# A GAT layer and a relational attention layer in one kernel: the order of the four score quads within a turn

## The chip, the cores and the metric

The kernel runs on one core of a Trainium2 chip. The metric is device time in microseconds (us) for one execution of the whole program. The program works in float32 throughout. The engines are called by the profile's names: PE (matmuls; PEld are its weight loads), DVE (vector), ACT (scalar activations), POOL (GpSimd) and SP, which here only issues DMAs.

## The reference, cut to what matters

64 graphs of 256 nodes with 256 features pass through two layers. Layer 0 is a graph attention (two attention steps, then a norm, a feed-forward of width 1024 and a norm); layer 1 is an attention with 8 heads whose weights pass through masks by relation, followed again by norm, feed-forward and norm.

```python
# layer 1, the part around the change (adj is 0 or 1 here, so two relations count)
q = (src @ Wq + bq), k = (src @ Wk + bk)          # 8 heads of 32
attn = softmax(einsum('bhid,bhjd->bhij', q, k) / sqrt(32))
for r in range(R):
    v_r = src @ Wv[r] + bv[r]
    out = out + einsum('bhij,bhjd->bhid', attn * (adj == r), v_r)
x = _ln(src + out @ Wo + bo, g1, beta1)
# layer 0's feed-forward, of the graphs that come next
h = _layernorm(residual + h, g_ln1, b_ln1)
ff = relu(h @ w_ff1 + b_ff1) @ w_ff2 + b_ff2
h = _layernorm(h + ff, g_ln2, b_ln2)
```

## The kernel before, in words

Two graphs are one group, so there are 32 groups. A stretch of the program, `turn(y_, x_, z)` (L1154), takes one group `y_` through the attention and the second feed-forward, the next group `x_` through its first feed-forward, and the one after that, `z`, through the two graph attention steps. The three are interleaved by hand. Inside a turn the order on PE, SP, DVE and ACT is the order of the Python calls (`tc.manual_schedule`, L1195, with all four engines while there is an `x_`); POOL is not among them. An engine executes in that order and waits where an input or a buffer isn't ready.

The steps that the change moves:

- **Scores, `scores(n)`** (L1164, in `weighted`, L1006). A quad is four heads of one graph; a turn has four: quads 0 and 1 for graph 0, quads 2 and 3 for graph 1. The 16 matmul instructions `sp` (L1015) contract over 32 rows each, so that four of them stand side by side in the rows of the array (32*128 in the profile); they write four PSUM banks. ACT then takes the exponential of each bank (L1021).
- **Masks and totals, `masks(n)`, `totals(n)`** (L1026, L1031): DVE multiplies the exponentials by the adjacency, two heads at a time, and adds both halves for the denominators.
- **Sums, `sums(n)`** (`applied`, L1034): 32 matmuls `po` (L1041) and 8 matmuls `zo` (L1044) with 32 output columns each, four side by side in the columns of the array (128*32). They need the masks, the totals and the values of their graph.
- **Values, `values`** (L992): per block of 128 nodes four matmul instructions of 512 columns (`vp`, L999), then a DVE add into `v` (L1001). Blocks 0 and 1 belong to graph 0, blocks 2 and 3 to graph 1.
- **Feed-forward steps, `first("2a 1a ...")`** (`hidden_seven`, L842, steps in L892). The first matrix product of the feed-forward is done with seven products (Strassen's way) for each half a and b of the hidden units. Steps 2, 5 and 3 use one PSUM bank (`h1b`) and are copied by ACT (L880); steps 1, 6, 7 and 4 use the other (`h1a`), the first three added by DVE (L883). Each step is four matmul instructions (L871). As they run in one bank one after the other, step 5a has to wait for the copy of 2a, 3a for the copy of 5a, 6a for the add of 1a, 7a for that of 6a, 4a for that of 7a. "r" and "s" are activations on ACT alone. Four subtractions (L854) on DVE prepare the moving operands; they wait for the DMAs `hT<-yt` (L687) that place the transposed features.
- **Shares, `shares(b)`** (`divided`, L1047): DVE transposes the denominators, inverts them, transposes back and multiplies `po` by them (L1052 to L1057); the PSUM tiles `po` and `zo` have one buffer each, so graph 1's sums wait for graph 0's shares.
- **`early(z)`** (L1064): a DVE transposition of the input of group `z`; **`project(z, ...)`** (L1074): its projection `xpp` on PE (L715), copied by ACT; **`plus(X["y"], rb1)`** (L839): the shift of the first norm, a DVE addition over 128x1024 elements; **`applied_norm(waiting...)`** (L818): four ACT activations (L828) after a small DVE one (L821), for the group that is leaving.

All matmul results but `po` and `zo` go to one rotating set of six PSUM banks (`bank`, L423): a new tile takes the bank that came free first and waits for its last reader.

Of the kernel before, what the change touches and what calls it, by code (L numbers as in the profile page):

```python
# [12 lines left out]
ALU = mybir.AluOpType  # L13
# [3 lines left out]
P = 128  # L17
# [368 lines left out]
def narrow_path(  # L386
# [13 lines left out]
    nc = tc.nc  # L400
    B, N, F = x.shape
# [7 lines left out]
    T = G * NB  # L409
# [13 lines left out]
    def bank(name):  # L423
        return psum.tile([P, 512], F32, tag="g", name=name, bufs=6)
# [4 lines left out]
    def load_x(u):  # L429


        xq = io.tile([P, KB, TN], F32, tag="xq", name=f"xq{u}", bufs=1)
        xu = x[G * u:G * (u + 1)].rearrange("b (n r) (k q c) -> q k r (b n) c", r=32, k=KB, c=32)
        for q in range(Q):
            for k in range(KB):
                nc.sync.dma_start(xq[q * 32:(q + 1) * 32, k, :].rearrange("r (n c) -> r n c", c=32), xu[q, k])
        g[u].update(xq=xq)
# [65 lines left out]
    def row(v, name, t=None):  # L503
        n = v.shape[0]
        if t is None:
            t = const.tile([P, n], F32, name=name)
        nc.sync.dma_start(t, bass.AP(tensor=v.tensor, offset=v.offset, ap=[[0, P], [1, n]]))
        return t
# [41 lines left out]
    rg1, rb1, rg2, rb2 = row(g_g1, "rg1"), row(g_b1, "rb1"), row(g_g2, "rg2"), row(g_b2, "rb2")  # L550
# [267 lines left out]
    def applied_norm(y, blocks, mv, rs, nm, part=None, gpsimd=False):  # L818
        bt = slice(blocks[0], blocks[0] + len(blocks))
        if part is None or part[0] == blocks[0]:  # L820
            nc.vector.scalar_tensor_tensor(nm[:, bt], mv[:, bt, 0], -1.0, rs[:, bt],  # L821
                                           op0=ALU.mult, op1=ALU.mult)
        for t in part or blocks:
            if gpsimd:
                nc.gpsimd.tensor_scalar(y[:, t, :], y[:, t, :], rs[:, t:t + 1], nm[:, t:t + 1],
                                        op0=ALU.mult, op1=ALU.add)
                continue
            mark["normed"] = nc.scalar.activation(y[:, t, :], y[:, t, :], AF.Identity,  # L828
                                                  bias=nm[:, t:t + 1], scale=rs[:, t:t + 1])
# [6 lines left out]
    def times(y, g_):  # L836
        nc.vector.tensor_mul(y, y, g_[:, None, :].to_broadcast(list(y.shape)))  # L837

    def plus(y, b_):  # L839
        nc.vector.tensor_add(y, y, b_[:, None, :].to_broadcast(list(y.shape)))  # L840
# [134 lines left out]
    def out_sums(u, l):  # L975
        two = [work.tile([P, HPB, NB * N], F32, tag=t, name=f"{t}q{u}_{l}") for t in ("e", "ea")]
        return [t[:, :, i * N:(i + 1) * N] for t in two for i in range(2)]
# [14 lines left out]
    def values(u, hT, blocks, v=None):  # L992
        if v is None:
            v = work.tile([P, T, 2 * F], F32, tag="v", name=f"v{u}", bufs=1)
        wvf = wv.rearrange("p c r f -> p c (r f)")
        for t in blocks:
            ps = bank(f"vp{u}_{t}")
            for k in range(KB):
                nc.tensor.matmul(ps, hT[k][:, t * P:(t + 1) * P], wvf[:, k, :],  # L999
                                 start=(k == 0), stop=(k == KB - 1))  # L1000
            nc.vector.tensor_tensor(v[:, t, :], ps, rbv, ALU.add)  # L1001
        return v
# [21 lines left out]
    def masked(b, m, ab, e, ea, pairs=(0, 2)):  # L1024
        for a in pairs:
            nc.vector.tensor_tensor(ea[:, a:a + 2, :], e[:, a:a + 2, :],  # L1026
                                    ab[:, None, :].to_broadcast([P, 2, NB * N]), ALU.mult)
# [19 lines left out]
    def divided(u, b, po, zo, oT):  # L1047


        rz = work.tile([P, KB * N], F32, tag="s" if u < NG - 1 else "yt", name=f"rz{u}_{b}", bufs=1)  # L1050
        rq = work.tile([P, KB * N // 32], F32, tag="rq", name=f"rq{u}_{b}")
        nc.vector.transpose(rz, zo)  # L1052
        nc.vector.reciprocal(rq, rz.rearrange("p (n r) -> p n r", r=32)[:, :, 0])  # L1053
        nc.gpsimd.tensor_add(low, low, rq)  # L1054
        nc.vector.transpose(rz.rearrange("p (n r) -> p n r", r=32),
                            rq[:, :, None].to_broadcast([P, KB * N // 32, 32]))
        mark[f"divided{b}"] = nc.vector.tensor_tensor(  # L1057
            oT[:, :, b * N:(b + 1) * N], po.rearrange("p (m n) -> p m n", m=KB),
            rz.rearrange("p (m n) -> p m n", m=KB), ALU.mult)
# [4 lines left out]
    def early(z):  # L1064

        d = g[z]
        xT = work.tile([P, KB, TN], F32, tag="hT", name=f"xT{z}")
        nc.vector.transpose(xT.rearrange("p k n -> p (k n)"), d["xq"].rearrange("p k n -> p (k n)"))
        d["xT"] = [xT[:, k] for k in range(KB)]
# [4 lines left out]
    def project(z, blocks=range(T)):  # L1074
        d = g[z]
        d["xp"] = projected(z, d["xT"], blocks, d.get("xp"))
# [73 lines left out]
    def piece():  # L1150
        if left:
            next(left[0], None)

    def turn(y_, x_, z):  # L1154
        Y, X, Z = (g.get(u) for u in (y_, x_, z))
        hT, y = Y["hT"], Y["y"]
# [3 lines left out]
        oT = q  # L1160
        acc = [None] * G
        e = {}

        def scores(n):  # L1164
            e[n] = weighted(y_, *quads[n], q, k_, Y["aT"])

        def masks(n, *pairs):
            masked(*e[n], *pairs)

        def totals(n):  # L1170
            e[n] = node_sums(*e[n])

        def sums(n):
            b, m = quads[n]
            if m == 0:
                acc[b] = [psum.tile([P, 512], F32, tag=t_, name=f"{t_}{y_}_{b}") for t_ in ("po", "zo")]
            applied(b, m, v, *e.pop(n), *acc[b])

        def shares(b):
            divided(y_, b, *acc[b], oT)  # L1180

        def out_(b):
            add_blocks(y_, "yop", y, b, lambda t, k: oT[:, k, t * P:(t + 1) * P],
# [2 lines left out]
        def first(names, ends=0):  # L1186

            if X:
                steps(names)
            else:  # L1190
                for _ in range(ends):
                    piece()
# [4 lines left out]
        with order:  # L1197
# [4 lines left out]
            last = norm(waiting[0][0], 3, waiting[0][1]) if waiting else None  # L1202
            key(0)
            key(1)
            if X:
                X["hT"] = normed_features(x_, 0, X["y"])
                times(X["y"], rg1)
            scores(0)
            if z + 1 < NG:
                load_x(z + 1)  # L1210
            if X:
                masks(0)
                totals(0)
            v = values(y_, hT, range(0, T // 2))
            if not X:
                masks(0)
                totals(0)
            if waiting:
                applied_norm(waiting[0][1], *last)
            if X:  # L1220
                v = values(y_, hT, range(T // 2, T), v)
            steps = first_hidden(x_) if X else None
            scores(1)
            if not X:
                v = values(y_, hT, range(T // 2, T), v)
            if Z:
                early(z)
            masks(1)
            totals(1)
            sums(0)  # L1230
            first("2a 1a 5a", 1)
            scores(2)
            sums(1)
            if X:
                shares(0)
            first("3a 6a", 1)
            if not X:
                with behind("out"):
                    shares(0)
            masks(2, (0,))  # L1240
            first("2b 1b")
            masks(2, (2,))
            first("5b 7a 3b ra 6b")
            totals(2)
            first("4a 7b rb")
            if X:
                plus(X["y"], rb1)
            scores(3)
            first("sa sb", 2)
            masks(3)  # L1250
            totals(3)
            if Z:
                project(z, range(0, T // 2))
            first("4b")
            sums(2)
            sums(3)
            if not Z:
                shares(1)
            if X:
                out = HiddenOut(x_, 0, X["y"], X["h1"], wf2s, out_sums(x_, 0))  # L1260
                if Z:
                    out.sums(1, 2)
            if Z:
                shares(1)
            out_(0)
            mv = moments(y_, 2, y, range(NB))
            piece()
# [2 lines left out]
            if Z:  # L1270
                early_adjacency(z)
            elif X:
                out.sums(1)
                out(1, 2)
                out.sums(2)
            out_(1)
# [21 lines left out]
            if X:  # L1298
# [3 lines left out]
                if Z:  # L1302
                    hT = normed_features(y_, 2, y, queues=(nc.sync, nc.scalar))
# [4 lines left out]
            if not Z:  # L1308
                piece()
                hT = to_features(y, f"h3T{y_}")  # L1310
                hT = [h.rearrange("p (t a r) -> p t a r", t=T, r=32) for h in hT]
# [52 lines left out]
            out = HiddenOut(y_, 1, y, h1, w2s, out_sums(y_, 1))  # L1364
# [26 lines left out]
    waiting = []  # L1391

    with tc.manual_schedule(engines={mybir.EngineType.PE, mybir.EngineType.SP}):
# [23 lines left out]
        first = HiddenOut(0, 0, g[0]["y"], g[0]["h1"], wf2s, out_sums(0, 0))  # L1417
# [63 lines left out]
```

## Time and profile before

| what | value |
|---|---|
| five runs, median (lowest to highest) | 3074.53 us (3073.17 to 3076.09) |
| the profiled execution | 3074.8 us |
| its span, from first to last instruction | 3073.2 us |
| granted clock of PE | 0.994 |
| PE / PEld / DVE / ACT / POOL busy | 3033.1 / 2330.7 / 2596.0 / 1601.1 / 642.6 us |
| one turn, first `qp` matmul to the next turn's | 93.43 us (for example 1321.09 to 1414.52) |

The profiled execution's own time lies 1.6 us above its span, and 0.3 us above the median. Times in the text such as 1328.05 are microseconds from the start of the span, in one turn in the middle of it. In the timeline a line gives the start, the time from the first start to the last end, the engine, the source line and the operation with its tiles, and in brackets how long the engine was idle before and who ended that. In the chain of waits a line gives the start and how long the chain ran through that piece of work. PE's matmuls overlap at their ends, so the distance from one block's start to the next one's is what a block costs.

### The profile page before, as it was taken

How to read it: one execution, taken by the hardware profiler on the slowest of the kernel's cores; microseconds unless marked ns; L12 is line 12 of the kernel's file. 1: busy time of each engine (PE TensorE's matmuls, PEld its weight loads, DVE VectorE, ACT ScalarE, POOL GpSimd, SP SyncE). 2: the span in 40 equal slices, each digit the busy share in tenths (PEclk: the TensorE clock that was granted, in tenths of full speed). 3: DMA queues.
4: the chain of work that ended last, by engine and by line, in shares of the span. 5: the costliest groups of instructions: out<-in, count | busy, mean ns of one | idle time of the engine just before them, and what ended most of it. 6: DMA issues, size and time to landing. Idle time of an engine off the chain costs nothing.

```text
span 3073.2 us, 56408 instructions
## 1 busy us (share of the span) xinstructions
PE 3033.1 (99%) x21432; PEld 2330.7 (76%) x21432; DVE 2596.0 (84%) x4886; ACT 1601.1 (52%) x3212; POOL 642.6 (21%) x888
## 2 busy tenths in 40 slices
PE   7999999999999999999999999999999999999998
PEld 6677877778777778777778777787777787777866
DVE  4788888888888888888888888888888888888876
ACT  4455555555545555545555455555455555555553
POOL 3122121222211221211221112222112212122200
PEclk8999999999999999999999999999999999999999
DMA  5011111221111211111211112111112111121000
GB/s 149 13 37 36 33 39 25 44 44 32 36 40 25 44 37 36 35 29 40 44 35 34 39 25 44 40 36 34 35 32 44 37 33 39 25 44 37 19 13 16
DMA packets 427988, 113.37 MB, mean 37 GB/s; under 512 B 364568, under 2 KB 427072, under 8 KB 427712
## 3 DMA queue, kind: packets, MB, share of 16 engines
q1 hardware_dynamic: 417664, 102.46, 15.8%
q10 hardware_dynamic: 8992, 6.19, 0.9%
q8 instruction: 172, 2.82, 0.4%
q0 software_dynamic: 1056, 1.05, 0.1%
q14 instruction: 104, 0.85, 0.1%
HBM read 57.04 MB, written 16.78 MB: 24 GB/s over the span
## 4 chain that ended last, share of the span: by engine, by line
PE 91%; DVE 7%; DMA 1%; ACT 1%; POOL 0%; issue 0%; SPq 0%; ACTq 0%; POOLq 0%; DVEq 0%
PE yf L960 22%; PE h1a L871 15%; PE h1b L871 11%; PE po L1041 8%; PE vp L999 7%; PE sp L1015 4%; PE xpp L715 4%; PE qp L986 4%; PE kp L986 4%; PE yop L786 4%; PE ygp L786 3%; PE hpp L775 2%; PE zo L1044 2%; DVE s L750 2%; DVE yt L668 1%; DVE eaq L946 1%
## 5 line engine op out<-in xcount | busy, mean ns | idle before, releaser
L880 ACT COPY h<-h1b 128x512 f32<-128x512 f32 x384 | 224.2, 584 | 390.9 <-PE h1b L871 390.9
L883 DVE TENSOR_TENSOR h<-h1a,h 128x512 f32<-128x512 f32 x384 | 263.6, 687 | 117.5 <-PE h1a L871 111.9
L828 ACT ACTIVATE y<-y,nm,rs 128x256 f32<-128x256 f32 x450 | 238.7, 591 | 238.3 <-DVE nm L821 234.0
L1026 DVE TENSOR_TENSOR ea<-e,aT 128x1024 f32<-128x1024 f32 x256 | 309.3, 1238 | 55.0 <-ACT e L1021 55.0
L1021 ACT ACTIVATE e<-sp 128x512 f32<-128x512 f32 x512 | 264.4, 604 | 52.0 <-PE sp L1015 48.7
L1054 POOL TENSOR_TENSOR low<-low,rq 128x16 f32<-128x16 f32 x64 | 13.8, 216 | 1088.6 <-DVE rq L1053 1088.6
L685 POOL COPY hT<-yt 32x256 f32<-32x256 f32 x244 | 206.2, 845 | 59.4 <-DVE yt L668 51.8
L968 DVE TENSOR_TENSOR y<-yf,y 128x256 f32<-128x256 f32 x448 | 183.1, 409 | 40.2 <-PE yf L960 40.1
L999 PE MATMUL vp<-wv,hT 128*128 128x512 f32 x480 | 214.0, 599 | 0.0
L801 DVE BATCH_NORM_STATS2 st<-y 128x6 f32<-128x256 f32 x512 | 207.8, 408 | 5.6
L812 POOL TENSOR_SCALAR rs<-mv 128x4 f32<-128x4 f32 (+1 forms) x130 | 31.2, 240 | 729.7 <-DVE mv L802 471.0
L999 PEld LDWEIGHTS vp<-wv,hT 128*128 128x128 f32 x480 | 88.7, 190 | 110.4 <-issue 103.2
L840 DVE TENSOR_TENSOR y<-y,rb 128x1024 f32<-128x1024 f32 (+1 forms) x130 | 166.5, 1281 | 3.2
L988 ACT ACTIVATE q<-qp,cols 128x512 f32<-128x512 f32 x64 | 44.0, 687 | 240.3 <-PE qp L986 240.3
L914 ACT ACTIVATE h<-h,cols 128x512 f32<-128x512 f32 x256 | 167.0, 714 | 1.5 <-DVE h L883 1.1
L837 DVE TENSOR_TENSOR y<-y,rg 128x1024 f32<-128x1024 f32 (+1 forms) x130 | 161.9, 1245 | 2.2 <-ACT y L828 1.1
L1031 DVE TENSOR_TENSOR es<-e 128x1024 f32<-128x1024 f32 x128 | 155.5, 1215 | 0.0
L677 POOL COPY hT<-yt 32x256 f32<-32x256 f32 x120 | 116.1, 968 | 169.5 <-DVE yt L668 165.7
L1015 PEld LDWEIGHTS sp<-q,k 32*128 32x128 f32 x2048 | 92.5, 184 | 72.1 <-issue 44.8
L1015 PE MATMUL sp<-q,k 32*128 32x256 f32 x2048 | 146.6, 400 | 0.0
L1041 PE MATMUL po<-e,v 128*32 128x256 f32 x2048 | 136.3, 384 | 0.0
L668 DVE STREAM_TRANSPOSE yt<-y 128x256 f32<-128x256 f32 x364 | 129.6, 412 | 7.4 <-ACT y L828 6.1
(249 smaller groups left out, 7196.5 us busy)
## 6 DMA issues: line engine op xcount, KB each, us to landing
hT<-yt SPq DMA_DIRECT2D x912, 32.0 KB, 2.0
y<-in_x_dram SPq DMA_DIRECT2D x32, 512.0 KB, 5.1
xq<-in_x_dram SPq DMA_DIRECT2D x240, 64.0 KB, 2.1
aq<-in_adj_dram SPq DMA_DIRECT2D x240, 64.0 KB, 2.4
out_dram<-y SPq DMA_DIRECT2D x30, 512.0 KB, 2.9
hT<-yt ACTq DMA_DIRECT2D x180, 32.0 KB, 1.9
wf<-in_L_gnn_w_ff_dram SPq DMA_DIRECT2D x2, 1024.0 KB, 7.1
w<-in_L_gnn_W_dram SPq DMA_DIRECT2D x2, 1024.0 KB
```

The lines of the kernel that those rows point to most:

```text
L786: nc.tensor.matmul(ps[:, i * F:(i + 1) * F], lhs(t, k), rhs(b, k), start=(k == 0), stop=(k == n - 1))
L828: mark["normed"] = nc.scalar.activation(y[:, t, :], y[:, t, :], AF.Identity, bias=nm[:, t:t + 1], scale=rs[:, t:t + 1])
L871: nc.tensor.matmul(ps[:, i * N:(i + 1) * N], w_[:, f * P:(f + 1) * P], m, start=first and i == 0, stop=True, skip_group_check=True)
L880: mark["copied"] = nc.scalar.copy(out(h, o, b), pair(ps))
L883: mark["added"] = nc.vector.tensor_tensor(out(h, o, b), pair(one[h]), out(h, o, b), ALU.add)
L960: nc.tensor.matmul(s.ps[n][:, i * F2:(i + 1) * F2], a[:, k, i * P:(i + 1) * P], w_[:, k, :], start=n in (1, 2, 5) and i == 0 and k == 0, s ...
L986: nc.tensor.matmul(ps, w[:, k, m * P:(m + 1) * P], hT[k], start=(k == 0), stop=(k == KB - 1))
L999: nc.tensor.matmul(ps, hT[k][:, t * P:(t + 1) * P], wvf[:, k, :], start=(k == 0), stop=(k == KB - 1))
L1015: nc.tensor.matmul(ps[a][:, j * N:(j + 1) * N], k_[hp, m, j0:j0 + P], q[hp, m, b * N:(b + 1) * N], start=True, stop=True)
L1021: mark[f"exp{b * KB + m}"] = nc.scalar.activation(e[:, a, :], ps[a], AF.Exp, scale=isd)
L1026: nc.vector.tensor_tensor(ea[:, a:a + 2, :], e[:, a:a + 2, :], ab[:, None, :].to_broadcast([P, 2, NB * N]), ALU.mult)
L1041: nc.tensor.matmul(po[hp, m * N:(m + 1) * N], vs[:, hp], w[:, a, j * N:(j + 1) * N], start=(n == 0), stop=(n == len(terms) - 1))
```

## The change

On PE, a turn that has both an `x_` and a `z` (30 of the 32) ran, from the first scores on: scores 0, values 0 to 3, scores 1, sums 0, steps 2a 1a 5a, scores 2, sums 1, steps 3a 6a 2b 1b 5b 7a 3b 6b 4a 7b, scores 3, two projections, step 4b, sums 2 and 3. It now runs: scores 0, values 0 to 2, scores 1, sums 0, scores 2, steps 2a 1a 2b 5a, values 3, steps 3a 6a, sums 1, scores 3, steps 5b 7a 1b 3b 6b 4a 7b, two projections, step 4b, sums 2 and 3.

On DVE, the totals, masks, the transposition of `early` and the shares take new places between the adds of the steps; the shares of graph 0 are split in two by a `yield`. The addition of `rb1` leaves DVE: POOL issues a DMA that adds `rb1` to `X["y"]` in SBUF, early in the turn. The group that is leaving gets its norm activations ahead of masks 0.

```diff
         nc.gpsimd.tensor_add(low, low, rq)
+        yield
         nc.vector.transpose(rz.rearrange("p (n r) -> p n r", r=32),
...
                 times(X["y"], rg1)
+                nc.gpsimd.dma_start(X["y"], rb1[:, None, :].to_broadcast([P, T, F]), accum_op=ALU.add)
             scores(0)
             if z + 1 < NG:
                 load_x(z + 1)
+            if waiting:
+                applied_norm(waiting[0][1], *last)
...
-                v = values(y_, hT, range(T // 2, T), v)
+                v = values(y_, hT, range(T // 2, T - 1), v)
             steps = first_hidden(x_) if X else None
             scores(1)
...
-            if Z:
-                early(z)
             masks(1)
-            totals(1)
+            if not X:
+                totals(1)
             sums(0)
-            first("2a 1a 5a", 1)
-            scores(2)
-            sums(1)
             if X:
-                shares(0)
-            first("3a 6a", 1)
-            if not X:
+                scores(2)
+                first("2a 1a")
+                totals(1)
+                first("2b")
+                masks(2, (0,))
+                first("5a")
+                v = values(y_, hT, range(T - 1, T), v)
+                first("3a 6a")
+                masks(2, (2,))
+                sums(1)
+                scores(3)
+                first("5b")
+                totals(2)
+                if Z:
+                    early(z)
+                first("7a 1b")
+                divide = shares(0)
+                next(divide)
+                first("ra 3b 6b")
+                next(divide, None)
+                first("4a 7b")
+                if Z:
+                    project(z, range(0, T // 2))
+                first("rb")
+                first("sa sb")
...
-            masks(2, (0,))
-            first("2b 1b")
-            masks(2, (2,))
-            first("5b 7a 3b ra 6b")
-            totals(2)
-            first("4a 7b rb")
-            if X:
-                plus(X["y"], rb1)
-            scores(3)
-            first("sa sb", 2)
             masks(3)
             totals(3)
-            if Z:
-                project(z, range(0, T // 2))
             first("4b")
             sums(2)
             sums(3)
```

The last two turns keep an order of their own: turn 30 has no `z`, so `early` and `project` fall away in it, and turn 31 has no `x_` either. After sums 3 the calls `out.sums(1)` and `out.sums(2)` now stand ahead of the second `shares` in every turn with an `x_`.

More of the change, by code (lines that the diff above doesn't have):

```diff
@@ L1179, in shares @@
         def shares(b):
-            divided(y_, b, *acc[b], oT)
+            return divided(y_, b, *acc[b], oT)
         def out_(b):
@@ L1217, in turn @@
                 totals(0)
-            if waiting:
-                applied_norm(waiting[0][1], *last)
             if X:
-                v = values(y_, hT, range(T // 2, T), v)
+                v = values(y_, hT, range(T // 2, T - 1), v)
             steps = first_hidden(x_) if X else None
@@ L1225, in turn @@
                 v = values(y_, hT, range(T // 2, T), v)
-            if Z:
-                early(z)
             masks(1)
-            totals(1)
+            if not X:
+                totals(1)
             sums(0)
-            first("2a 1a 5a", 1)
-            scores(2)
-            sums(1)
             if X:
-                shares(0)
-            first("3a 6a", 1)
-            if not X:
-                with behind("out"):
-                    shares(0)
-            masks(2, (0,))
-            first("2b 1b")
-            masks(2, (2,))
-            first("5b 7a 3b ra 6b")
-            totals(2)
-            first("4a 7b rb")
-            if X:
-                plus(X["y"], rb1)
-            scores(3)
-            first("sa sb", 2)
+                scores(2)
[23 more added lines that the diff above has]
+                first("sa sb")
+            else:
+                piece()
+                scores(2)
+                sums(1)
+                piece()
+                with behind("out"):
+                    for _ in shares(0):
+                        pass
+                masks(2)
+                totals(2)
+                scores(3)
+                piece()
+                piece()
             masks(3)
             totals(3)
-            if Z:
-                project(z, range(0, T // 2))
             first("4b")
@@ L1256, in turn @@
             sums(3)
-            if not Z:
-                shares(1)
             if X:
                 out = HiddenOut(x_, 0, X["y"], X["h1"], wf2s, out_sums(x_, 0))
+                out.sums(1)
                 if Z:
-                    out.sums(1, 2)
-            if Z:
-                shares(1)
+                    out.sums(2)
+            for _ in shares(1):
+                pass
             out_(0)
@@ L1272, in turn @@
             elif X:
-                out.sums(1)
                 out(1, 2)
```

## The prediction

> **What bounds the kernel now.** I read the page's busy times first, then the chain of waits, then PE's and DVE's timelines in one turn.
>
> ```profile
> PE 3033.1 (99%) x21432; PEld 2330.7 (76%) x21432; DVE 2596.0 (84%) x4886; ACT 1601.1 (52%) x3212; POOL 642.6 (21%) x888
> ...
> PE 91%; DVE 7%; DMA 1%; ACT 1%; POOL 0%; issue 0%; SPq 0%; ACTq 0%; POOLq 0%; DVEq 0%
> ```
>
> PE is busy for 99% and is 91% of the chain that ended last. DVE at 84% is no bound; it counts only where PE waits for one of its results. So a change of order can win or lose just two things: what PE loses between blocks, and PE's short waits. The chain of waits in one turn shows both (start, length, block):
>
> ```profile
> 1328.12 1.08 PE sp L1015 x16
> 1329.20 7.06 PE vp L999 x16
> 1336.26 1.08 PE sp L1015 x16
> 1337.34 1.86 PE po L1041 x32
> 1339.20 0.43 PE zo L1044 x8
> 1339.63 1.06 PE h1b L871 x4
> 1340.69 0.86 PE h1a L871 x4
> 1341.56 0.94 PE h1b L871 x4
> 1342.50 1.08 PE sp L1015 x16
> ...
> 1352.28 2.85 PE h1a L871 x12
> 1355.12 1.08 PE sp L1015 x16
> 1356.20 1.95 PE xpp L715 x8
> ```
>
> A feed-forward step costs 0.86 where nothing disturbs it. The first one behind `zo` costs 1.06. Sixteen scores, four abreast, are also four steps of work (0.86) and cost 1.08. The 32 `po` behind scores cost 1.86; the same 32 behind another quad's `zo` cost 1.73 (at 1361.31). The projection costs 1.95 behind scores and 1.75 elsewhere (at 1365.39). So each time PE goes from one division of the array to another it loses about 0.20 into a full-array block, 0.13 into `po` and 0.22 into scores.
>
> The second loss: step 5a takes 0.94, and so do 5b and 3b; each waits for an ACT copy of its bank, and its weights load late (0.08 each). Steps 6b, 4a and 7b take 2.85 in place of 2.59: 7b waits for DVE's add of 6b (0.25).
>
> **The change part by part**, for one turn, 30 of which have the full new order.
>
> *Divisions of the array.* Before, the stretch from scores 0 to the output product enters scores 4 times, `po` 3 times and full blocks 5 times (values, 2a, 3a, projection, output product). After, scores 2 and 3 follow `zo` directly: scores are entered 4 times, `po` 3 times, full blocks 4 times (values, 2a behind scores 2, 5b behind scores 3, output product). One entry goes: **-0.20**. This assumes that scores cost 1.08 behind `zo` as they do behind a full block. The trace has no scores directly behind `zo`. Bounds: 0.86, their bare work, if that entry is free (-0.22 each), and 1.30, twice the entry, if both divisions had to be paid (+0.22 each); two such places, so -0.44 to +0.44 a turn. I take 1.08, the nearest row: scores cost it in all four places, whatever stood ahead.
>
> *Values 3 behind scores 1.* Scores 1 come 1.72 sooner (4 of 16 matmuls, 6.88 / 4). Four of six banks are needed. In the order in which banks come free these are those of scores 0 (heads 1 to 3) and that of values 0, where before they were heads 2 and 3 and values 0 and 1. DVE frees it late:
>
> ```profile
> 1327.91 1.23 DVE L837 TENSOR_TENSOR y<-y,rg 128x1024 f32<-128x1024 f32 x1
> 1330.33 2.56 DVE L1026 TENSOR_TENSOR ea<-e,aT 128x1024 f32<-128x1024 f32 x2 [1.20 <-ACT e L1021]
> 1332.82 1.21 DVE L1031 TENSOR_TENSOR es<-e 128x1024 f32<-128x1024 f32 x1
> 1333.96 1.27 DVE L1001 TENSOR_TENSOR v<-vp,rbv 128x512 f32<-128x512 f32 x2
> ```
>
> Values 0 are added from 1333.96 to 1333.96 + 0.68 = 1334.64 (0.68 is the single add of L1001). PE would be ready for scores 1 at 1336.19 - 1.72 = 1334.47 and, with some 0.05 from DVE's end to PE's start (at 7b DVE ends at 1353.93 and PE's weights start at 1353.99), begins at 1334.69: **+0.21**. All of PE stands behind it. Bounds: 0 if the add is that much sooner; 0.8 if the bank is values 1's, added 0.6 later.
>
> *Waits of the steps.* I laid the new order out with the durations above: every instruction starts when its engine is free and its inputs are there. Scores 2 start at 1338.05 and their four exponentials (0.49 apart) hold ACT to 1341.0; the copy of 2a ends at 1341.6. Step 2b now stands ahead of 5a, which is due at 1341.8: its weights load late (0.07). Later 3b and 6b each load late by 0.07 to 0.09, 7b still waits 0.25 for the add of 6b. Sum 0.48; before 0.08 + 0.08 + 0.08 + 0.25 = 0.49. **About 0.** Values 3 stand in front of 3a and take its wait away.
>
> *DVE.* `plus` (1.22) goes; the rest is the same work in new places. DVE ends totals 3 at about 1360.6, against 1360.9 before, and sums 3 want them only at 1363, so nothing is gained: scores 3's exponentials and the step adds set its pace. The shares of graph 0 end at 1356.6, sums 2 need them at 1358.9. The subtractions wait for the DMAs `hT<-yt` until 1337.42 as before; step 2a, which reads the same tile, comes at 1339.1, so a cover of 1.7 is left. Ahead of masks 0 stands a new DVE instruction of 0.15, in DVE's 1.20 of idle time. **0.**
>
> *ACT.* The projection's copies now stand ahead of "rb" and "s", which end some 0.6 later; behind them wait the sums `eq` on DVE and graph 1's shares, done at 1366.2; the output product that reads them starts at 1366.98. **0**, cover 0.7.
>
> *SP.* Its queue holds the next load of `xq` until `early` has read the buffer: 1340.16 now, some 10 us later after. The next entries are wanted 30 us later. **0.**
>
> *The accumulating DMA.* Its sum is read by the first add of the feed-forward's output, over 35 us later; the only DMAs that POOL issues before took 8.1 us to land. Hidden. But POOL must issue it, behind its four copies (1327.99 to 1330.7), beside DVE's masks 0. That masks pair took 2.56, with the copies beside its first half (1.43); the pair at 1340.05, alone, took 2.31. The two POOL issues in the trace take 1.0 and 0.8. So between 0 and +0.22 on masks 0, and on scores 1 as they wait for values 0 behind them. I take 0: the copies read and write 256 elements on each of 32 partitions, an issue moves no tile.
>
> The Trainium skill, SBUF — State Buffer, section "Who interferes with whom", says that a DVE instruction with two SBUF inputs contends with a GpSimd instruction that reads SBUF, not with one that only writes it; the copies agree (0.39 alone, 1.38 beside the multiplication by `rg`). If making the descriptors is only writing, the term is 0 by the page; if it also reads, the page would have it as the +0.22 above.
>
> Sum: -0.20 + 0.21 + 0 = +0.01 a turn, 0.3 us over 30 turns. In turn 30 nothing stands between 7b and 4b any more, which costs about 1 us, and the missing `plus` gives about as much back where DVE is the bound there. The profiled execution (3074.8, span 3073.2 + 1.6) gives 3075.1; the median of the runs is 0.3 lower. I say **3075.0**.
>
> **The rivals.** About 0.2% (6 us, 0.2 a turn) is what a measurement of this kernel can tell from no change.
>
> *Faster.* Scores behind `zo` cost less than behind a full block, or DVE frees the bank in time. For it: into `po` PE loses only 0.13, so entries differ. Against: 1.08 at every place. With half the entry saved (-0.11 twice) and no wait at scores 1 the sum is -0.20 - 0.22 = -0.42, times 30 is -13: **3062**. Either one alone gives 3068 to 3069.
>
> *Slower: DVE is late at values 0.* POOL's issue stretches masks 0 by 0.22, PE waits 0.43 instead of 0.21 at scores 1, 30 x 0.22 = 6.6: **3082**. It decides once values 0's add ends after 1334.47, which it already does here, so every delay counts in full. With values 1's bank, +0.6 a turn: 3093.
>
> *Slower: the divisions are dear.* 1.30 for scores behind `zo`: 30 x 0.44 = 13: **3088**. It is in the range's upper end.
>
> *The order isn't what the diff says.* On PE, DVE and ACT it is written out by hand; only POOL's place for its DMA is free. I give this nothing.
>
> **How the numbers follow.** No change that can be told (3069 to 3081) 0.46; faster 0.32 (the best known term is a saving, the added waits are each a matter of 0.1 to 0.2); slower 0.22 (late DVE 0.15, dear divisions or another bank 0.07). The range leaves out half of each far case: 3062 to 3084. The likeliest case's own range is 3069 to 3081.
>
> **What would show it.** In PE's timeline: 1.08 from scores 2's start to 2a's, with 2.29 ahead of it from `po` to scores; the entry behind `zo` read off as any excess. A wait of 0.2 ahead of scores 1, with DVE's L1001 as its releaser. L840 gone from the group of 130 by about 31, a DMA issued by POOL in each turn, where the trace now has two in all. Masks 0 at 2.56 again, or longer. A turn of 93.4. The prediction is wrong if scores behind `zo` differ from 1.08 by over 0.1, if scores 1 wait 0 or over 0.4, or if 5a waits for ACT's copy by over 0.2.

## The result and the profile after

The changed kernel took 3081.1 us (median of 23 runs, 3077.4 to 3083.5); before, run beside it, 3075.1 (43 runs, 3071.9 to 3077.5). The ratio is 1.0020, 95% interval 1.0014 to 1.0025: **slower by 6.0 us, 0.2%**, at the border between "no change" and "slower". The forecast was 3075.0 with a range of 3062 to 3084. The profiled execution took 3082.5, its span is 3080.8; the granted clock of PE is 0.994, as before.

From the page of the kernel after, busy times and the chain's shares:

```profile
PE 3034.5 (98%) x21432; PEld 2339.8 (76%) x21432; DVE 2560.2 (83%) x4855; ACT 1601.0 (52%) x3212; POOL 684.3 (22%) x919
...
PE 87%; DVE 8%; ACT 1%; DMA 1%; SPq 1%; POOL 1%; issue 1%; DVEq 0%; ACTq 0%; POOLq 0%
```

DVE has lost 35.8 us and 31 instructions: `plus` is gone. POOL has gained 41.7 us and 31: the issues of the DMA. PE's work is the same, but SP's queue and POOL now appear in the chain that ended last, each with 1%. The chain of waits of the kernel after, in the turn from 1327.14 to 1420.67 (start, length, block):

```profile
1340.60 1.27 PE sp L1015 x14
1341.87 1.86 PE po L1041 x32
1343.73 0.43 PE zo L1044 x8
1344.16 1.08 PE sp L1015 x16
1345.24 1.06 PE h1b L871 x4
...
1347.16 1.87 PE h1b L871 x8
...
1358.64 1.01 PE h1b L871 x4
1359.64 2.89 PE h1a L871 x12
```

Scores directly behind `zo` cost 1.08, and the step behind them 1.06, as behind any other block. Scores 1 cost 1.27: a wait of 0.19 inside them (the chain's line counts 14 of their 16 matmuls). The pairs and triples of steps have their small waits: 1.87 where two steps' bare work is 1.72, 1.01 for 0.86, 2.89 for 2.59. This turn is 93.53 long, before 93.44; most turns are like it. DVE's timeline in the same turn, masks 0 and the adds of values 0 to 2:

```profile
1336.38 2.57 DVE L1026 TENSOR_TENSOR ea<-e,aT 128x1024 f32<-128x1024 f32 x2 [0.93 <-ACT e L1021]
...
1340.01 1.87 DVE L1001 TENSOR_TENSOR v<-vp,rbv 128x512 f32<-128x512 f32 x3
```

Masks 0 are as long as before. The first add begins at 1340.01 and takes 0.68, to 1340.69, while scores 1 are on PE from 1340.53 on.

In ten of turns 1 to 29, and in turn 30, step 2a starts late. Here is one of these, the turn from 1233.07 to 1327.14, in the chain and then in DVE's timeline (in brackets the idle time before and its releaser):

```profile
1250.09 1.08 PE sp L1015 x16
1251.17 0.65 issue
1251.82 1.10 PE h1b L871 x4
```

```profile
1251.70 0.42 DVE L854 TENSOR_TENSOR tt<-hT 128x256 f32<-128x256 f32 x1 [3.89 <-DMA hT<-yt]
```

PE stands still for 0.65, and DVE has waited 3.89 for the transposed features. They landed just before both could start. The chain calls PE's gap "issue", a time for which it found no releaser; DVE's line, 0.12 earlier and about the same tile, names it. In the totals of this line over the whole trace DVE's idle time behind `hT<-yt` goes from 20.9 us (24 times) to 101.6 (44 times). Most of that costs nothing, as DVE has less to do there without `plus`: in dma_later below it is 63.6 (44 times), and no step 2a comes late. SP's timeline shows where the delay begins. First the kernel before, then the kernel after, each with the twelve issues of one turn as one line (first start, time to the last end); then POOL's timeline of the kernel after, in the same turn:

```profile
1328.01 7.55 SPq L687 DMA_DIRECT2D hT<-yt  x12
```

```profile
1334.06 9.16 SPq L687 DMA_DIRECT2D hT<-yt  x12
```

```profile
1334.04 2.70 POOL L685 COPY hT<-yt 32x256 f32<-32x256 f32 x4 [0.23 <-DVE yt L668]
1336.69 1.35 POOL L1209 DMA_DIRECT2D y<-rb  x1
```

Twelve issues take 9.16 where they took 7.55. One by one, as medians over turns 1 to 28: each lasts 0.59 before; after, the eighth and the ninth last 1.10, and they begin 11.35 and 12.51 into the turn. POOL's issue runs from 9.55 to 10.90, and the accumulating DMA lands at 14.83. So two of SP's issues stretch while that DMA moves its 512 KB. The last issue comes at 14.94 instead of 13.88, and the subtractions start at 17.57 (up to 18.63) instead of 16.15; step 2a is due at 18.03.

### The profile page after: what moved, and what is told of

Its sections match the earlier page's. It is cut to its first block, busy times and chain, and to the rows that moved or that the text cites. A ratio compares the mean times of both kernels' runs of the same rounds, so it can differ in the third digit from the quotient of the medians.

```text
span 3080.8 us, 56471 instructions
## 1 busy us (share of the span) xinstructions
PE 3034.5 (98%) x21432; PEld 2339.8 (76%) x21432; DVE 2560.2 (83%) x4855; ACT 1601.0 (52%) x3212; POOL 684.3 (22%) x919
## 4 chain that ended last, share of the span: by engine, by line
PE 87%; DVE 8%; ACT 1%; DMA 1%; SPq 1%; POOL 1%; issue 1%; DVEq 0%; ACTq 0%; POOLq 0%
PE yf L960 21%; PE h1a L871 14%; PE h1b L871 11%; PE po L1041 7%; PE vp L999 7%; PE sp L1015 4%; PE yop L786 4%; PE xpp L715 4%; PE ygp L786 3%; PE qp L986 3%; PE kp L986 3%; PE hpp L775 2%; PE zo L1044 2%; DVE s L750 2%; DVE eaq L946 1%; DVE yt L668 1%
## 5 line engine op out<-in xcount | busy, mean ns | idle before, releaser
L1015 PE MATMUL sp<-q,k 32*128 32x256 f32 x2048 | 153.0, 400 | 1.2 <-ACT k L988 1.2
L717 ACT COPY xp<-xpp 128x260 f32<-128x260 f32 x128 | 48.0, 375 | 195.7 <-PE xpp L715 195.7
L854 DVE TENSOR_TENSOR tt<-hT 128x256 f32<-128x256 f32 x122 | 51.4, 421 | 105.7 <-DMA hT<-yt 101.6
```

The costliest lines, as they stand in the source:

```text
L1015: nc.tensor.matmul(ps[a][:, j * N:(j + 1) * N], k_[hp, m, j0:j0 + P], q[hp, m, b * N:(b + 1) * N], start=True, stop=True)
```

## The experiments

Theory 1 in the expectations: the accumulating DMA holds up the transfers of `hT`, and 2a waits for them. Theory A: scores 1 wait for the bank of values 0 because totals 0 stand ahead of their add on DVE. All kernels side by side; "turn" is the usual (median) turn of turns 1 to 29, "long" the number of turns over that by more than 0.12 us, the next two columns are medians from the start of a turn, "turn 30" is its length:

| kernel | time | ratio to before on the same chip | turn | long | last `hT` issue | subtractions | turn 30 |
|---|---|---|---|---|---|---|---|
| before | 3075.1 | 1 | 93.44 | 5 | 13.88 | 16.15 | 74.12 |
| after | 3081.1 | 1.0020 (1.0014 to 1.0025) | 93.53 | 7 | 14.94 | 17.57 | 75.60 |
| plus_on_dve | 3077.5 | 1.0008 (0.9999 to 1.0017) | 93.55 | 1 | 13.89 | 16.20 | 75.22 |
| totals_later | 3077.3 | 1.0006 (0.9997 to 1.0015) | 93.35 | 11 | 14.94 | 17.61 | 75.82 |
| both | 3072.1 | 0.9991 (0.9982 to 1.0000) | 93.34 | 2 | 13.90 | 16.24 | 75.02 |
| dma_alone | 3077.6 | 1.0005 (0.9996 to 1.0014) | 93.44 | 8 | 14.98 | 17.23 | 74.17 |
| scores3_apart | 3080.6 | 1.0010 (1.0001 to 1.0019) | 93.53 | 1 | 13.89 | 16.23 | 75.21 |
| values_back | 3103.1 | 1.0085 (1.0070 to 1.0100) | 94.27 | 1 | 13.89 | 16.95 | 75.95 |
| shares_at_once | 3105.4 | 1.0093 (1.0078 to 1.0109) | 94.33 | 4 | 13.90 | 16.24 | 75.99 |
| last_as_before | 3073.4 | 0.9989 (0.9980 to 0.9998) | 93.33 | 3 | 13.90 | 16.24 | 74.14 |
| dma_later | 3072.7 | 0.9989 (0.9980 to 0.9998) | 93.33 | 3 | 13.89 | 16.21 | 74.17 |

The kernel before took 3075.3 beside plus_on_dve to dma_alone, 3076.6 beside scores3_apart to last_as_before, and 3076.1 beside dma_later. The first 102 to 107 us, ahead of turn 0, differ by that much between single traces although the code there is the same; so turns, and not spans, are compared.

**plus_on_dve**: the kernel after, with `rb1` added by DVE, in its idle time ahead of the subtractions.

```diff
-                nc.gpsimd.dma_start(X["y"], rb1[:, None, :].to_broadcast([P, T, F]), accum_op=ALU.add)
...
                 v = values(y_, hT, range(T // 2, T - 1), v)
+                plus(X["y"], rb1)
```

> The changed kernel without the accumulating DMA: rb1 is added by DVE again (1.22 us), in DVE's idle time between the add of values 2 and the four subtractions. Theory 1 (the DMA holds up the hT DMAs, and 2a waits for them): SP's twelfth hT issue, 14.94 us after the turn's first qp in the changed kernel, goes back to 13.88 as before, the subtractions start at 16.2 in place of 17.6, no turn has scores 2 to step 2a longer than 1.08 (the changed kernel: up to 1.79, in 12 of 30 turns over 1.08), and the time falls by 2 to 3 us, to 3078 to 3079. Theory 2 (all of the loss is the new order of PE's steps): the turn is the same 93.53, the longer turns were chance, and the time stays at 3081 within 1.

3077.5: 3.6 us less. The issues and the subtractions are back where they were before, one long turn is left of seven, and step 2a is late in none (in the kernel after it is late in eleven of turns 0 to 30, where the expectation says twelve of 30). The usual turn keeps its length. So the DMA cost some 2 to 4 us in this order, only in the turns with a late 2a.

**totals_later**: the kernel after, with totals 0 behind the adds of values 0 and 1 on DVE.

```diff
                 masks(0)
-                totals(0)
             v = values(y_, hT, range(0, T // 2))
+            if X:
+                totals(0)
```

> The changed kernel, with totals 0 on DVE behind the adds of values 0 and 1 in place of ahead of them. Theory A (scores 1 wait for the bank of values 0, which DVE frees late): values 0's add ends at 12.4 in place of 13.55, scores 1's 16 matmuls take 1.08 in place of 1.27, the typical turn is 93.53 - 0.2 = 93.33, and the time falls by 6 us, to 3075. Theory B (the 0.2 at scores 1 has another cause, such as the weights of q and k, or is covered by a later wait of the steps): scores 1 stay at 1.27, or the turn stays at 93.5 and 3a, 6b or 7b wait longer; the time stays at 3081 within 1.

The usual turn falls by 0.18, to 93.35: the wait at scores 1 is gone. The add of values 0 ends 12.42 into the turn instead of 13.55. The time falls by 3.8 and not by 5.7, because 2a now comes at 17.83 and meets late features more often: 11 long turns instead of 7, ten of them with a late 2a. The mechanism held, and part of its gain went into the other wait.

**both**: the two together.

> Both edits together: rb1 added by DVE in its idle time, totals 0 behind the adds of values 0 and 1. If the two losses are separate, they add: 3081 - 6 - 2.5 = 3072 to 3073, which is faster than the kernel before by 2 to 3 us, with a typical turn of 93.33 and no long turns from scores 2. If the DMA and the bank share a cause or DVE becomes the bound with the addition back (totals 0 needed by zo of sums 0): 3075 to 3081.

3072.1, 9.0 less than the kernel after, with turns of 93.34 and two long ones. Both losses are gone, about as forecast (3072 to 3073). The two are not independent: singly the edits gave 3.6 and 3.8, 7.4 in all, since an earlier 2a loses more to the late features as long as the DMA is there. Against totals_later the DMA cost 5.2. Scores 1 in the chain of waits of this kernel, a turn in the middle:

```profile
1331.93 1.08 PE sp L1015 x16
```

1.08 in place of 1.27.

**dma_alone**: the kernel before, with the DMA in place of `plus` and nothing else.

```diff
                 times(X["y"], rg1)
+                nc.gpsimd.dma_start(X["y"], rb1[:, None, :].to_broadcast([P, T, F]), accum_op=ALU.add)
...
-            if X:
-                plus(X["y"], rb1)
```

> The kernel before, with only the addition of rb1 moved from DVE to the accumulating DMA, issued where the changed kernel issues it. Theory 1 (the DMA holds up the hT DMAs by 1 to 1.5 us): the twelfth issue goes to 14.9, the subtractions start at 17.6, DVE's masks 1 and totals 1 behind them come later and sums 1 wait in the turns where the DMAs are latest: slower by 1 to 8 us than the kernel before. Theory 2 (the DMA is hidden): the same time as before within 1 us, since DVE isn't the bound.

2.3 us more, with an interval that includes no change (0.9996 to 1.0014), so the time alone decides little. The trace does: the last issue at 14.98 and the subtractions at 17.23 in the old order too. The DMA does this, not the order of PE. In the trace the stretch from scores 2 to step 3a, which is 3.37 in every turn before, is 0.3 to 0.7 longer in five turns, 2.1 in all: sums 1, which stand in it, are held up, as forecast. The usual turn stays at 93.44.

The next four start from **both**, the version in which the two losses are mended.

**scores3_apart**: step 5b between sums 1 and scores 3, so that one quad's scores no longer stand directly behind sums.

```diff
-                scores(3)
                 first("5b")
+                scores(3)
```

> As the version with both mends (3072.1 us, turn 93.34), but step 5b now stands between sums 1 and scores 3. Theory: each entry from one division of the array into full blocks costs PE about 0.20, and scores cost the same 1.08 behind a full block as behind sums; so one more entry is paid: a turn of 93.54, and 30 x 0.20 = 6 us: 3078. Rival (scores behind sums save nothing, the gain of the version with both mends came from elsewhere): turn 93.34, 3072. A second rival, that 5b behind sums instead of behind scores also spares or adds a wait of its own, would show as a change of the step waits in PE's rows, not of the 0.20 at the entry.

The usual turn is 93.53, 0.19 more; the time is 7.2 above last_as_before on the same chip, of which turn 30 is 1.1. The chain of waits, first of **both**, then of this kernel:

```profile
1345.48 0.43 PE zo L1044 x8
1345.91 1.08 PE sp L1015 x16
1346.98 1.06 PE h1b L871 x4
1348.04 1.73 PE h1a L871 x8
```

```profile
1352.40 0.43 PE zo L1044 x8
1352.84 1.06 PE h1b L871 x4
1353.90 1.08 PE sp L1015 x16
1354.97 1.92 PE h1a L871 x8
```

5b costs 1.06 and scores 1.08 in either order; the steps behind cost 1.92 instead of 1.73, the entry into full blocks that was spared. So one entry into full blocks costs 0.19 a turn, 5.7 us over 30 turns; that entry is what the order itself saves.

**values_back**: values 3 ahead of scores 1 again.

```diff
-                v = values(y_, hT, range(T // 2, T - 1), v)
+                v = values(y_, hT, range(T // 2, T), v)
...
                 first("5a")
-                v = values(y_, hT, range(T - 1, T), v)
                 first("3a 6a")
```

> As the version with both mends (3072.1 us), but values 3 stand ahead of scores 1 again, so that 3a follows 5a directly. Theory (values 3 cover the copy of 5a's bank): 2b behind 1a shows that such a copy is done about 0.9 after its step's matmuls; with nothing between 5a and 3a, 3a waits about 0.8 to 0.9: a turn of about 94.2, 30 x 0.85 = 25 us: 3097. Rival (3a takes another buffer or the copy is fast enough, values 3 only fill): no change, 3072.

94.27 a turn, 0.93 more, where 0.85 was expected; the time is 29.6 above last_as_before. Its chain of waits between 5a and 3a:

```profile
1355.64 1.88 PE h1b L871 x8
...
1357.55 0.59 ACT h L880
...
1358.19 1.13 PE h1b L871 x4
```

3a waits 0.65 (0.59 and two short gaps in the chain, 0.02 and 0.04) for ACT's copy, and with its weights loaded late it costs 1.13 instead of 0.86: 0.92 together. Values 3 cover that.

**shares_at_once**: graph 0's shares not split.

```diff
                 divide = shares(0)
-                next(divide)
+                for _ in divide:
+                    pass
                 first("ra 3b 6b")
-                next(divide, None)
```

> As the version with both mends (3072.1 us), but all four DVE instructions of graph 0's shares stand ahead of the add of step 6b. In that version DVE ends the reciprocal at 1351.4 of a turn in the middle, and the second transposition and the product took 1.35; the add of 6b, which began at 1351.79, would begin at about 1352.8. Theory (the add of 6b is the last thing 7b waits for): 7b waits 1.0 longer, 30 x 1.0 = 30 us: 3102, a turn of 94.3. Rival (DVE has room there, the split is worth nothing): 3072.

94.33 a turn, 0.99 more; 1.0 was expected; the time is 32.0 above last_as_before. DVE's timeline in this kernel:

```profile
1367.88 0.71 DVE L1056 STREAM_TRANSPOSE rz<-rq 128x512 f32<-128x512 f32 x1
1368.63 0.69 DVE L1058 TENSOR_TENSOR q<-po,rz 128x512 f32<-128x512 f32 x1
1369.24 0.68 DVE L883 TENSOR_TENSOR h<-h1a,h 128x512 f32<-128x512 f32 x1
```

The add of 6b comes behind the whole division, and PE's 7b starts at 1369.97, when it has ended. The `yield` is worth 30 us by itself.

**last_as_before**: in turn 30, which has no projection, scores 3 stand between 7b and 4b as they did before.

```diff
-                scores(3)
+                if Z:
+                    scores(3)
                 first("5b")
...
                 first("rb")
+                if not Z:
+                    scores(3)
```

> As the version with both mends (3072.1 us), but in turn 30, which has no projection to put between 7b and 4b, scores 3 stand there as they did before. Theory (turn 30 lost 1.1 to 1.7 us in the new order because 4b waits for 7b's add there): turn 30 is again about 74.1 long in place of 75.0 to 75.8, the whole about 1 us shorter: 3071. Rival (turn 30 is longer for another reason, the place of out.sums): 75 again, 3072. The difference is too small for the times; turn 30 itself in the trace decides.

Turn 30 is 74.14 long, as before the change. Turn 30 of the kernel after, in its chain of waits, shows what the new order did there:

```profile
2952.06 0.69 DVE h L883
2952.75 0.63 DVE rz L1056
...
2953.40 0.69 DVE q L1058
2954.09 0.61 DVE h L883
...
2954.74 1.13 PE h1a L871 x4
```

Step 4b waits for DVE's add of 7b, and ahead of that stands the second half of the shares (1.34). In the other turns the projection hides it.

**dma_later**: last_as_before with the accumulating DMA again, now behind graph 0's shares on POOL.

```diff
-                plus(X["y"], rb1)
...
+                nc.gpsimd.dma_start(X["y"], rb1[:, None, :].to_broadcast([P, T, F]), accum_op=ALU.add)
                 out = HiddenOut(x_, 0, X["y"], X["h1"], wf2s, out_sums(x_, 0))
...
-                                            ("PE", "SP", "DVE", "Activation")[:4 if X else 2]})
+                                            ("PE", "SP", "DVE", "Activation", "Pool")[:5 if X else 2]})
```

> As the version with both mends and turn 30 as before (3073.4 us where before took 3076.6; turn 93.33), but rb1 is added by the accumulating DMA again, now issued behind graph 0's shares, some 32 us into the turn, well after the transfers of hT (POOL's order is written out for this; two of its small instructions change places by it). Theory (the DMA cost time only because it ran beside the twelve hT transfers, holding up SP's last issue from 13.9 to 14.9 and the subtractions from 16.2 to 17.6): last issue 13.9 and subtractions 16.2 again, no wait ahead of 2a, turn 93.33, time the same as that version, ratio to before 0.999. Rival (the DMA costs time wherever it stands, through POOL's issue beside DVE's instructions or through other transfers it meets): a typical turn over 93.45, or as many long turns as with the early DMA, and 3 us or more above that version.

3072.7, ratio 0.9989 (0.9980 to 0.9998), within the runs' spread the same as with `plus` on DVE. POOL issues the DMA 33.5 us into the turn, for 1.36 again, and it lands at 38.7. SP's twelve issues in this kernel's timeline:

```profile
1327.56 7.54 SPq L687 DMA_DIRECT2D hT<-yt  x12
```

7.54, as before the change. Once it no longer runs beside the transfers of `hT`, the same DMA costs nothing that the turns or these times show.

## Why the prediction missed by 6 us, point by point

The result lies within the stated range, but by the range's width: none of the reasons given for a slower kernel (masks 0 stretched, dear divisions, another bank) occurred. The 3088 that the prediction places in the range's upper end lies above its 3084.

*Divisions: right.* Scores behind `zo` cost 1.08, as taken; both bounds, 0.86 and 1.30, are out. scores3_apart measures the entry spared as 0.19 against 0.20.

*Values 3 behind scores 1: right.* A wait of 0.19 against 0.21, for the bank of values 0, with the cause named: totals_later takes it away. One detail differs: scores 1 begin at once, and it is a bank inside the block that comes late (1.27 long, no gap ahead). That 3a's wait goes was right as well (values_back, 0.93).

*Waits of the steps: mis-sized.* 0.48 was forecast, "About 0" against before. From the distances of the starts in PE's timeline it is 0.59: 2b 0.04, 5a 0.10, 1b 0.04, 3b 0.10, 6b 0.05, 7b 0.26. That is 0.1 a turn more, 3 us in all. It accounts for the difference between the usual turn forecast (+0.01) and measured (+0.09), and the order's own net gain is therefore 0.10 a turn, as the turn of **both** shows, and not 0.20.

*The accumulating DMA: this step failed.* It was called "Hidden", with only its issue on POOL as a risk, and the subtractions were taken to start "as before", so that "a cover of 1.7 is left" ahead of 2a. I asked who reads its result and whom its issue disturbs, and not which transfers run beside its 512 KB. The subtractions start 1.42 later, of which 1.05 are the stretched issues. Of the cover 0.46 is left in the middle, and nothing in ten of turns 1 to 29. In those, sums 2 start later by 2.2 us in all (from the trace: 0.41, 0.21, 0.33, 0.24, 0.53, 0.09 and 0.38 in seven turns; in the other three the delay is taken up again). plus_on_dve and dma_later take the delay away in two ways, dma_alone brings it into the old order.

The Trainium skill, DMA: Bandwidth & Descriptors, section "Issuing engines are not separate DMA queues", says that DMAs of SP, ACT and GpSimd run on the same 16 DMA engines and interleave. These traces fit that in part: with POOL's DMA under way, what waits for SP's starts at 17.57 against 16.15. But 1.05 of these 1.42 are time of SP's own issues, which is not the interleaving that the sentence speaks of.

*POOL's issue beside masks 0: right, nothing.* The slower rival "DVE is late at values 0" did not happen. Masks 0 took 2.57 against 2.56 before, with POOL's issue (1336.69 to 1338.04) wholly beside them; the median over turns 1 to 28 is 2.57 in both, and in plus_on_dve, which has no such issue. The measurement decides for the reading of the section "Who interferes with whom" by which the term is 0.

*Turn 30: half right.* It was to lose about 1 us because nothing stands between 7b and 4b, and to get it back through the missing `plus`. It lost 1.48 (75.60 against 74.12). 0.9 of this is the place of scores 3 (75.02 in both, 74.14 in last_as_before), where 4b waits behind the second half of the shares; 0.4 goes with the DMA (75.22 in plus_on_dve), whose late 2a meets this turn too, and 0.2 with the wait at scores 1. Nothing came back: in the kernel before, `plus` does not stand in the chain of waits there. The other change in this turn, one call of `out.sums` placed ahead of the second `shares`, shows no cost, as last_as_before keeps it; in the turns with a `z` both calls stood there before the change as well.

*Sum.* 0.09 x 30 = 2.7, the waits of 2a 2.2, turn 30 1.5: 6.4, against 6.0 measured. The forecast's 0.3 lacked all three. The agreement is looser than it looks: all traces also have long turns without a late 2a (five in the trace before, 1.8 us in all, one in the trace after, 0.4), and what causes them was not tried. In these two traces turns 0 to 30 together differ by 5.5, from 2881.6 to 2887.1.

The **faster** rival needed two things, a cheaper entry and no wait at scores 1. The second can be had by moving one DVE instruction; the first did not show.

## What to carry to other kernels

A DMA whose result is wanted late is not free: look which other transfers are under way from its issue to its landing, and who waits for those. Here the same DMA cost 2 to 5 us beside them, and nothing that shows 24 us later. When PE's order is tightened, list for each block the bank it takes and the engine that frees it, and put that engine's less urgent work (here totals 0) behind the freeing instruction; the order's 0.1 a turn showed only when that was done. And a cover that is worked out from the old trace holds only as long as nothing in the change touches what ends it.

## What the runs showed of the hardware that was not expected

SP's own issue instruction takes longer while an accumulating DMA of POOL moves data: 1.10 instead of 0.59 for two of twelve, in the medians of 28 turns, in the kernel after and in dma_alone (1.08 and 1.14 there); 0.57 to 0.59 for all twelve in plus_on_dve, both and dma_later. POOL's issue has ended (10.90) when the first of the two begins (11.35). Whether a DMA of this size that doesn't accumulate would do the same was not tried. Some 0.4 more is lost between the last issue and the subtractions. Which part of the issue it is that waits, no view shows. The accumulating DMA of 512 KB took 1.35 to issue and landed 5.3 us (median) after its issue began; the two plain ones of that size that POOL issues in the trace before, at the start of the program beside many other loads, took 8.1.
